# A new order of blocks and a sum that stays out of TensorE in layer 0 of a four-layer sparse graph network

## The chip, the cores and the metric

The kernel runs on one core of one Trainium2 chip. The metric is the device time of one execution in microseconds, from the first to the last instruction and what lies around them; lower is better. Engines are called PE (TensorE), DVE (VectorE), ACT (ScalarE), POOL (GpSimd) and SP (SyncE) in the profile.

## The reference

Four layers of graph attention run over 4096 nodes with 256 features each. An adjacency matrix of 4096 by 4096 integers says who is whose neighbour; it is symmetric, has ones on its diagonal, and each row has only a handful of ones.

```python
h = relu(layernorm(x));  x = x + L0(h, adj)   # 4 heads of 64, then elu
h = relu(layernorm(x));  x = x + L1(h, adj)   # 1 head, h @ W + att @ h
h = relu(layernorm(x));  x = x + L2(h, adj)   # 4 heads
h = relu(layernorm(x));  x = x + L3(h, adj)   # 4 heads, q k v

def L0(h, adj):
    Wh = (h @ W).reshape(n, 4, 64)
    e = leaky_relu(s_i[:, None] + s_j[None, :], 0.2)   # s_i, s_j: Wh times two vectors
    alpha = softmax(where(adj == 0, -inf, e), axis=1)
    return elu(einsum('ijh,jhd->ihd', alpha, Wh).reshape(n, 256))
```

## The kernel before

The kernel works on lists of neighbours instead of the matrix. Its first part (`lists`) scans the matrix, makes a list of up to 24 neighbours for every node, and sorts the nodes by the length of their lists. The sorted nodes lie in 32 blocks of 128, one node to a partition. `CAPS` gives the most neighbours that a node of each block may have: 23 in block 0, 14 in block 1, down to 3 in block 31.

Layer 0 begins inside that first part: while the matrix is scanned, the first 6 neighbours (`EARLY`) of every node are fetched and summed (`early`). What is left of layer 0 is its late part, which `layer(0)` runs once all lists are there. `slots(0, b)` is `CAPS[b] - 6`, at least 0: 17, 8, 7, 6, 6, 5, 5 for blocks 0 to 6, 4 for 7 to 9, 3 for 10 to 14, 2 for 15 to 18, 1 for 19 to 22, and 0 for blocks 23 to 31. Those last nine have no late neighbours: their early sum only has to be divided by the sum of its weights.

`layers` calls `reload` and then `layer` for each of the four layers. `reload` has SyncE load, one after the other: the lists of blocks 0 and 1, the lists of blocks 30 and 31, the rows (`rx`: features, early sum, its greatest score, its source score and the sum of its weights, 262 KB a block) of the first four blocks in the order of work, the lists of blocks 2 to 29, and the rows of the other 28 blocks. VectorE then makes three small tables from the lists (L708, L715, L717).

The order of work is written out by hand: within these functions each engine runs its instructions in the order of the program, and only semaphores make one engine wait for another. `layer` goes through the blocks in `ORDER`: 0, 31, 1, 30, 2, 29 and so on, a long list and a short one in turn. In each of its 32 steps:

- `fill` issues on GpSimd the gathers (L755) of the blocks up to four steps ahead (`AHEAD`), one gather of 128 rows for each slot, into a ring buffer. A gather of layer 0 reads the table of layer 0.
- `scores` (L913 to L952) makes the weights of the block's neighbours on VectorE, with the exponential on ScalarE. It does nothing for a block without slots.
- `weigh` (L974 to L1042) takes the sum. For a block with slots VectorE multiplies its own early sum (L1014) and the gathered rows (L1028) by their weights, and TensorE adds them up in PSUM by matmuls with the identity (L1019, L1038). A float32 matmul stands in the profile as two instructions. For a block without slots only L977 (reciprocal), L1014 and L1019 are left.
- `settle` of the block two steps back: ScalarE takes the exponential of the sum (L1052, L1053), VectorE makes elu of it and adds x (L1063, L1064), then the statistics of the next layer norm (L569, L570, L576).
- the norm of the block three steps back: four small VectorE instructions (L579 to L585), relu on ScalarE (L732), transposes on TensorE (L740), a copy on ScalarE (L742) and the product with layer 1's weights on TensorE (L748).
- `third` of the block four steps back: VectorE adds the product to x (L1080), ScalarE copies two small pieces (L1081, L1082), and GpSimd sends the rows to the table of layer 1 (L765).

In a step the program order is: gathers, exponential of the block two back, norm of the one three back, scores of this one, third of the one four back, rest of the settlement, product, weigh. GpSimd's queue holds gathers and sends in that order. Layer 1 gathers from the whole table of layer 1, so its first gather follows layer 0's last send.

Of the kernel before, what the change touches and what calls it, by code (L numbers as in the profile page):

```python
# [9 lines left out]
F32 = mybir.dt.float32  # L10
# [4 lines left out]
ALU = mybir.AluOpType  # L15
# [4 lines left out]
P = 128  # L20
D = 256
# [27 lines left out]
WL = W + TOPK  # L49

ORDER = [b for k in range(16) for b in (k, 31 - k)]

RING = 36 * 512
AT_ONCE = 8
# [15 lines left out]
class Sparse:  # L70
# [614 lines left out]
    def reload(self):  # L685

        nc, tc, nt, n = self.nc, self.tc, self.nt, self.n
        by_place = self.placed.rearrange("(b p) k -> p b k", p=P)
        near = self.near = self.big.tile([P, nt, 32], U32, name="s_near")
        for a, b in ((0, 2), (nt - 2, nt), (2, nt - 2)):  # L690
            back = nc.sync.dma_start(
                out=near[:, a:b, 0 : TOPK + 1],
                in_=by_place[:, a:b, OWN : OWN + TOPK + 1].bitcast(U32),
            )
            if a == 0:
                for i in self.sent:
                    tc.add_manual_dep(
                        back.ins, i.name,
                        mybir.DependencyInfo(
                            mybir.DependencyClass.Sync, mybir.DependencyReason.DATA  # L700
                        ),
                        reason="every row",
                    )
            for k in {0: [], nt - 2: ORDER[:4], 2: ORDER[4:]}[a]:
                nc.sync.dma_start(out=self.rx[k], in_=self.placed[ts(k, P), 0:OWN])

        self.own_f = self.big.tile([P, nt], F32, name="s_own_f")
        nc.vector.tensor_copy(self.own_f, near[:, :, TOPK])  # L708

        where = self.big.tile([P, nt], F32, name="s_place_of")  # L710
        nc.gpsimd.iota(
            where, pattern=[[P, nt]], base=0, channel_multiplier=1,
            allow_small_or_imprecise_dtypes=True,
        )
        nc.vector.tensor_copy(near[:, :, TOPK - 1], where)  # L715
        self.away = self.big.tile([P, nt, TOPK], F32, name="s_away")
        nc.vector.tensor_scalar(  # L717
            self.away, near[:, :, 0:TOPK], float(n), FAR, ALU.is_ge, ALU.mult
        )
# [86 lines left out]
    def layer(self, l):  # L806


        nc, nt, vs = self.nc, self.nt, {}
        wide = (W, WL, W, 2 * D)[l]  # L810
        slots = RING // wide
        ring = self.ring[:, : slots * wide].rearrange("p (k w) -> p k w", w=wide)
        todo, held, at = list(ORDER), {}, 0
        made = []

        def fill(i):
            nonlocal at
            while todo and nt - len(todo) <= i + AHEAD:
                j = todo[0]
                K = self.slots(l, j)  # L820

                room = K + (K % 2 if l > 1 else 0)
                s = (at if at + room <= slots else 0) if K else 0
                if any(s < e and b < s + room for b, e in held.values()) or (
                    l == 3 and len(held) > 3
                ):
                    return
                todo.pop(0)
                if l == 3:
                    vs[j] = self.pool.tile([P, D], F32, name=f"s_vself_{j}", tag="vself", bufs=5)  # L830
                    nc.sync.dma_start(out=vs[j], in_=self.tab[3][ts(j, P), D:])
                k0 = EARLY if l == 0 else 0
                for k in range(K):
                    at_k = self.near[:, j, k0 + k : k0 + k + 1]
                    self.fetch(ring[:, s + k, :], self.tab[l], at_k)
                held[j] = (s, s + room)
                at = s + room if K else at

        sums, behind, turning, rows = {}, {}, {}, {}

        def settle(c, parts=(0, 1)):

            if 0 in parts and c in sums:
                behind[c] = self.settle(l, c, sums.pop(c), made)
                next(behind[c])
            if 1 in parts and c in behind:
                next(behind[c])

        def norm(d):

            if l < 3 and d in behind:
                turning[d] = self.turned(self.pool, next(behind.pop(d)), f"{l + 1}_{d}")
                next(turning[d])

        def product(d):
            if d in turning:
                rows[d] = self.advance(l + 1, d, next(turning.pop(d)), made)
                next(rows[d])

        def third(d):  # L860
            if d in rows:
                next(rows.pop(d), None)
            for send in made:
                self.send(*send)
            made.clear()

        S, N = (0, 1) if l == 1 else (2, 3)
        for i in range(nt):
            fill(i)
            b, c, d, e = (ORDER[k] if k >= 0 else None for k in (i, i - S, i - N, i - N - 1))  # L870
            if S:
                settle(c, (0,))
            norm(d)
            g = ring[:, held[b][0] : held[b][1], :]
            p = self.scores(l, b, self.rows[b], g[:, : self.slots(l, b), :])
            third(e)
            if S:
                settle(c, (1,))
            product(d)
            sums[b] = self.weigh(l, b, vs.pop(b) if l == 3 else self.rows[b][:, 0:D], g, p)  # L880
            del held[b]
            if not S:
                settle(b)
        z, y, x, w = ORDER[-1:-5:-1]
        if S:
            settle(y)
            norm(x)
            third(w)
            product(x)
            settle(z)  # L890
            norm(y)
            third(x)
            product(y)
        norm(z)
        third(y)
        product(z)
        third(z)
# [72 lines left out]
    def weigh(self, l, b, me, g, p):  # L970

        nc, pool = self.nc, self.pool
        H = 1 if l == 1 else 4
        K = self.slots(l, b)  # L974
        tot = pool.tile([P, H], F32, name=f"s_t_{l}_{b}", tag="t", bufs=3)
        if K == 0:
            nc.vector.reciprocal(tot, self.before[b])  # L977
            mine = tot
        else:
            by_head = p[:, : K + 1, :].rearrange("p k h -> p h k")  # L980
            if l == 0:
                was = pool.tile([P, H], F32, name=f"s_was_{b}", tag="was", bufs=2)
                nc.vector.tensor_tensor(was, p[:, K, :], self.before[b], ALU.mult)
                nc.vector.tensor_reduce(tot, by_head[:, :, :K], AX.X, ALU.add)
                nc.vector.tensor_tensor(tot, tot, was, ALU.add)
            else:
                nc.vector.tensor_reduce(tot, by_head, AX.X, ALU.add)  # L987
            nc.vector.reciprocal(tot, tot)  # L988
            nc.vector.tensor_tensor(  # L989
                by_head, by_head, tot.unsqueeze(2).to_broadcast([P, H, K + 1]), ALU.mult  # L990
            )
            mine = p[:, K, :]
# [15 lines left out]
        if pairs and not full:  # L1008
            mev = g[:, K, v0 : v0 + D]
        else:  # L1010
            mev = pool.tile([P, D], F32, name=f"s_me_{l}_{b}", tag="me", bufs=3)
        if full:
            nc.vector.tensor_scalar(mine, mine, 0.5, None, ALU.mult)  # L1013
        nc.vector.tensor_tensor(  # L1014
# [121 lines left out]
class Net:  # L1136
# [341 lines left out]
    def dot_attention(self, wq, bq, wk, bk, wv, bv):  # L1478
        nc, tc, nt, n, nb = self.nc, self.tc, self.nt, self.n, self.nb
        scale = 1.0 / 8.0  # L1480
        with ExitStack() as ctx:
# [88 lines left out]
            for b in range(nb):  # L1570
# [45 lines left out]
                while waiting:  # L1616
                    weigh()
# [58 lines left out]
```

## Time and profile before

| | |
|---|---|
| three timed runs | 1837.8, 1838.98, 1839.6 us; median 1838.98 |
| the profiled execution | 1841.32 us, span 1839.6 us |
| busy: PE, DVE, ACT, POOL | 994.8, 1379.9, 423.7, 1184.8 us |
| late part of layer 0: first gather issued | 432.3 us |
| late part of layer 0: last send issued | 655.5 us |
| layer 1: first gather issued | 658.8 us |
| DVE, PE, ACT, POOL busy from 430 to 660 | 153, 129, 78, 123 us |

All times inside the execution are counted from the start of the span. Busy time is the sum over instructions, an average over stages that have different limits, so a stage has to be looked at by itself. In the lines of a timeline the first number is the start, the second the length in us; square brackets hold the idle time of the engine before it and what ended it. An instruction of a form such as `128x256 f32` works on 128 partitions with 256 float32 each.

### The profile page before, as it was taken

The numbers are of one execution on the slowest core, as the hardware profiler recorded it, in microseconds if no ns is written. First come the engines' busy times: TensorE is split into PE (matmuls) and PEld (weight loads), VectorE is DVE, ScalarE is ACT, GpSimd is POOL, SyncE is SP. The second block draws the span as 40 slices with busy tenths as digits, with TensorE's granted clock in tenths as the row PEclk, the third lists the DMA queues.
The fourth block names the chain that finished last, engine by engine and source line by source line (L and its number), as shares of the span: only waits on it lengthen the run. The fifth ranks groups of instructions, "written<-read, shape, count | busy, mean of one in ns | idle before, by whom it ended". The sixth has DMA issues, their size and how long they took to land. (4 is left out here: it accounts for less than half of the span.)

```text
span 1839.6 us, 14362 instructions
## 1 busy us (share of the span) xinstructions
PE 994.8 (54%) x2569; PEld 481.7 (26%) x2569; DVE 1379.9 (75%) x3900; ACT 423.7 (23%) x1240; POOL 1184.8 (64%) x1324
## 2 busy tenths in 40 slices
PE   4878787750666611222232167788785344565555
PEld 3523232220455400111111023343342111221122
DVE  6899989850688808888888257888885587887777
ACT  5864435000244401111111002222222000000000
POOL 1067756676566357777776477777772577776774
PEclk9988889875788855555555588889987676777777
DMA  9899877348533134444444344444443577666763
GB/s 319 281 394 363 287 259 254 97 148 242 168 87 88 51 84 128 131 132 130 132 132 121 69 111 133 134 135 131 136 131 97 156 215 210 208 208 181 209 205 108
DMA packets 123017, 312.89 MB, mean 170 GB/s; under 512 B 31236, under 2 KB 49671, under 8 KB 122920
## 3 DMA queue, kind: packets, MB, share of 16 engines
q0 software_dynamic: 68064, 207.46, 39.7%
q1 hardware_dynamic: 54856, 104.44, 16.2%
q14 instruction: 73, 0.60, 0.1%
q8 instruction: 24, 0.39, 0.1%
HBM read 276.80 MB, written 35.00 MB: 169 GB/s over the span
## 5 line engine op out<-in xcount | busy, mean ns | idle before, releaser
L755 POOL DMA_INDIRECT s_ring<-s_tab,s_near x924 | 883.8, 956 | 356.7 <-issue 190.4
L1033 PE MATMUL s_acc<-s_ring,s_ident 128*128 128x512 f32 x588 | 319.5, 697 | 183.3 <-issue 95.0
L1033 PEld LDWEIGHTS s_acc<-s_ring,s_ident 128*128 128x128 f32 x588 | 130.5, 228 | 368.2 <-issue 245.5
L755 POOL DMA_INDIRECT s_g<-s_tab,s_keep x192 | 183.2, 954 | 64.3 <-issue 57.0
L483 DVE MAX8 s_cand<-s_pt 128x8 f32<-128x256 f32 x512 | 181.6, 417 | 16.4 <-PE s_pt L481 15.9
L1028 DVE TENSOR_TENSOR s_ring<-s_ring,s_shares 128x2048 f32<-128x2048 f32 (+7 forms) x121 | 187.5, 1573 | 0.0
L740 PE MATMUL s_pht<-s_ident,s_h 128*128 128x128 f32 x128 | 34.3, 361 | 248.0 <-ACT s_h L732 248.0
L748 PE MATMUL s_ps<-s_we_l,s_ht 128*128 128x264 f32 x256 | 113.4, 586 | 79.2 <-ACT s_ht L742 79.2
L999 DVE SCALAR_TENSOR_TENSOR s_acc<-s_ring,s_p,s_acc 128x256 f32<-128x256 f32 x277 | 135.7, 490 | 9.7
L261 ACT ACTIVATE s_low<-s_raw 128x1024 fp8e4<-128x1024 int32 x128 | 134.2, 1050 | 21.3 <-DMA s_raw<-in_adj_dram 18.1
L556 PE MATMUL s_ae<-s_g,s_ident 128*128 128x512 f32 x192 | 113.7, 688 | 36.5 <-DVE s_g L547 36.5
L913 DVE TENSOR_TENSOR s_e<-s_ring,s_rx 128x8 f32<-128x8 f32 (+12 forms) x87 | 15.7, 181 | 148.0 <-DMA s_ring<-s_tab,s_near 143.0
L476 PE MATMUL s_pt<-s_low,s_mark 128*128 128x512 fp8e4 x256 | 107.7, 421 | 34.3 <-DVE s_cand L483 15.0
L748 PE MATMUL s_ps_kv<-s_wkv,s_ht 128*128 128x512 f32 x128 | 82.9, 782 | 73.6 <-ACT s_ht L742 73.6
L932 DVE TENSOR_TENSOR s_ring<-s_ring,s_shares 128x2048 f32<-128x2048 f32 (+7 forms) x48 | 81.1, 1690 | 47.8 <-DMA s_ring<-s_tab,s_near 31.5
L481 PE MATMUL s_pt<-s_places,s_stands 128*128 128x512 bf16 x256 | 106.5, 416 | 1.4 <-DVE s_stands L453 1.4
L952 ACT ACTIVATE s_shares<-s_e 128x32 f32<-128x32 f32 (+8 forms) x87 | 17.4, 200 | 387.8 <-DVE s_e L945 340.2
L575 ACT ACTIVATE s_y<-s_mv,s_eps 128x1 f32<-128x1 f32 x96 | 28.3, 294 | 294.0 <-DVE s_mv L570 294.0
L740 PEld LDWEIGHTS s_pht<-s_ident,s_h 128*128 128x128 f32 x128 | 18.3, 172 | 287.9 <-ACT s_h L732 271.9
L748 PEld LDWEIGHTS s_ps<-s_we_l,s_ht 128*128 128x128 f32 x256 | 63.0, 272 | 110.0 <-ACT s_ht L742 100.1
L935 DVE TENSOR_REDUCE s_e<-s_ring 128x32 f32<-128x2048 f32 (+7 forms) x48 | 81.2, 1692 | 1.7
L1021 PE MATMUL s_acc<-s_me,s_ident 128*128 128x512 f32 x60 | 42.8, 803 | 70.8 <-DVE s_me L1014 67.2
(193 smaller groups left out, 1673.4 us busy)
## 6 DMA issues: line engine op xcount, KB each, us to landing
s_raw<-in_adj_dram SPq DMA_DIRECT2D x128, 512.0 KB, 7.8
s_ring<-s_tab,s_near POOLq DMA_INDIRECT x924, 3.0
s_rx<-s_placed SPq DMA_DIRECT2D x32, 262.0 KB, 8.0
s_tab<-s_kv SPq DMA_DIRECT2D x32, 256.0 KB, 2.8
s_tab<-s_keep SPq DMA_DIRECT2D x8, 528.0 KB, 6.8
s_tab<-s_rx SPq DMA_DIRECT2D x32, 132.0 KB, 2.3
s_keep<-in_x_dram SPq DMA_DIRECT2D x8, 512.0 KB, 4.1
s_vself<-s_tab SPq DMA_DIRECT2D x32, 128.0 KB, 2.9
```

The costliest lines, as they stand in the source:

```text
L261: nc.scalar.activation(low[r][:, ts(h, n // 4)], raw.pop(q), AF.Copy, saturate=False, accum_out=self.sums[:, r, h : h + 1],)
L476: nc.tensor.matmul(pt, lhsT=self.mark, rhs=lo[:, ts(g, IB)], start=True, stop=False)
L481: nc.tensor.matmul(pt, lhsT=self.stands[:, g, :], rhs=self.places, start=False, stop=True)
L483: nc.vector.max(out=cand[:, g * (IB // CH) + k, :], in_=pt[:, ts(k, CH)])
L556: nc.tensor.matmul(acc, lhsT=self.ident, rhs=g[:, :, k, 0:D], start=False, stop=(k == E - 1))
L748: self.nc.tensor.matmul(ps[:, :width], lhsT=ht[:, c, :], rhs=w[:, c, :], start=(c == 0), stop=(c == KC - 1),)
L755: return self.nc.gpsimd.indirect_dma_start(out=out, out_offset=None, in_=table[:, :], in_offset=bass.IndirectOffsetOnAxis(ap=idx, axis=0),)
L932: nc.vector.tensor_tensor(kq, kq, q.unsqueeze(1).to_broadcast([P, m, D]), ALU.mult)
L935: nc.vector.tensor_reduce(e[:, k0 : k0 + m, :], kq.rearrange("p k (h d) -> p k h d", h=4), AX.X, ALU.add)
L999: nc.vector.scalar_tensor_tensor(acc, g[:, k, 0:D], p[:, k, :], acc, ALU.mult, ALU.add)
L1028: nc.vector.tensor_tensor(v, v, p[:, k0 : k0 + m, :].unsqueeze(3).to_broadcast([P, m, H, D // H]), ALU.mult)
L1033: nc.tensor.matmul(both, lhsT=self.ident, rhs=g[:, k : k + 2, v0 : v0 + D], start=(k == 0 and not full), stop=(k + 2 >= K),)
```

## The change

Layer 0's late part gets an order of its own, `FIRST`: 31, 30, 29, 28, 0, then 27, 1, 26, 2, 25, 3 and so on to 15, 13, and 14 at the end. The other layers keep `ORDER`. The rows are loaded in the new order too, five of them instead of four ahead of the lists of blocks 2 to 29. A block without slots no longer goes through TensorE: `weigh` returns the product of L1014 in SBUF, and `settle` reads it there. The buffer of these products has four places instead of three, since such a block holds its place until `settle` is done. The early return also skips `self.turns += 1` (L995), so `turns`, which picks one of two halves of the PSUM tile for the weights (L951), counts only blocks with slots in layer 0.

```diff
 ORDER = [b for k in range(16) for b in (k, 31 - k)]
+
+FIRST = [31, 30, 29, 28, 0] + [b for k in range(1, 14) for b in (28 - k, k)] + [14]
...
-            for k in {0: [], nt - 2: ORDER[:4], 2: ORDER[4:]}[a]:
+            for k in {0: [], nt - 2: FIRST[:5], 2: FIRST[5:]}[a]:
                 nc.sync.dma_start(out=self.rx[k], in_=self.placed[ts(k, P), 0:OWN])
...
-        todo, held, at = list(ORDER), {}, 0
+        order = ORDER if l else FIRST
+        todo, held, at = list(order), {}, 0
...
-            b, c, d, e = (ORDER[k] if k >= 0 else None for k in (i, i - S, i - N, i - N - 1))
+            b, c, d, e = (order[k] if k >= 0 else None for k in (i, i - S, i - N, i - N - 1))
...
-        z, y, x, w = ORDER[-1:-5:-1]
+        z, y, x, w = order[-1:-5:-1]
...
         if K == 0:
+
             nc.vector.reciprocal(tot, self.before[b])
-            mine = tot
+            mev = pool.tile([P, D], F32, name=f"s_me_{l}_{b}", tag="me", bufs=4)
+            nc.vector.tensor_tensor(
+                mev.rearrange("p (h d) -> p h d", h=H), me.rearrange("p (h d) -> p h d", h=H),
+                tot.unsqueeze(2).to_broadcast([P, H, D // H]), ALU.mult,
+            )
+            return mev
...
-            mev = pool.tile([P, D], F32, name=f"s_me_{l}_{b}", tag="me", bufs=3)
+            mev = pool.tile([P, D], F32, name=f"s_me_{l}_{b}", tag="me", bufs=4)
```

## The prediction

> **What bounds the kernel now.** I read the page first. VectorE is busy 75% of the span, more than any other engine, but that is an average over the list building and four layers, and the chain that ended last covers only the last 32 us (from 1807.6). So I cut the stage that the change touches, layer 0's late part, into windows.
>
> ```profile
> 443.00:464.00 21.00, 0.00 (x0) 0.00 (x0) 0.49 (x2) 0.00 (x0) 14.77 (x16) 0.50 0.99 271
> 464.00:480.00 16.00, 11.98 (x38) 9.24 (x38) 8.41 (x21) 0.57 (x2) 12.23 (x13) 0.66 0.91 325
> 520.00:540.00 20.00, 12.86 (x55) 9.72 (x56) 18.14 (x72) 10.06 (x38) 12.10 (x13) 0.99 0.31 88
> 620.00:640.00 20.00, 12.43 (x48) 9.13 (x47) 18.21 (x83) 9.74 (x36) 3.90 (x4) 0.88 0.09 31
> ```
>
> The columns are length, then busy us of PE, PE weight load, VectorE, ScalarE, GpSimd, the granted TensorE clock, the DMA share and GB/s. From 520 to 640 VectorE is busy 18 of each 20 us and the rest is gaps between instructions: it is the bound. From 443 to 464 it does nothing while GpSimd issues gathers and the DMA engines are full. The timeline of VectorE says what it waits for (start, length, then idle time before and releaser):
>
> ```profile
> 442.81 0.56 DVE L717 TENSOR_SCALAR s_away<-s_near 128x768 f32<-128x768 uint32 x1
> 463.88 0.23 DVE L913 TENSOR_TENSOR s_e<-s_ring,s_rx 128x68 f32<-128x68 f32 x1 [20.51 <-DMA s_ring<-s_tab,s_near]
> 480.53 0.43 DVE L1063 SCALAR_TENSOR_TENSOR s_ex<-s_ex,s_rx 128x256 f32<-128x256 f32 x1 [7.32 <-ACT s_ex L1053]
> 494.45 0.42 DVE L1080 TENSOR_TENSOR s_rx<-s_rx,s_ps 128x256 f32<-128x256 f32 x1 [3.92 <-PE s_ps L748]
> 517.57 0.42 DVE L1080 TENSOR_TENSOR s_rx<-s_rx,s_ps 128x256 f32<-128x256 f32 x1 [2.68 <-PE s_ps L748]
> ```
>
> 20.5 us go by until block 0's 17 gathers have landed, 7.3 us until ScalarE has block 0's sum, which waits for TensorE, and 3.9 and 2.7 us for TensorE's product. Later waits are small (0.55, 0.39, 0.39) until the tail. TensorE's own timeline explains three of them:
>
> ```profile
> 469.21 10.42 PE L1038 MATMUL s_acc<-s_ring,s_ident 128*128 128x256 f32 x34 [0.86 <-DVE s_ring L1028]
> 485.81 6.77 PE L1038 MATMUL s_acc<-s_ring,s_ident 128*128 128x256 f32 x16 [1.50 <-DVE s_ring L1028]
> 522.62 2.86 PE L1038 MATMUL s_acc<-s_ring,s_ident 128*128 128x256 f32 x12 [0.69 <-DVE s_ring L1028]
> ```
>
> Block 0's sum takes 10.4 us, and block 1's 16 instructions take 0.42 us each where a later block's 12 take 0.24: the granted clock is 0.50 until about 474, 1.00 from 476 to 483, and 0.50 again from 486 to 492. GpSimd's timeline gives the stage's two ends:
>
> ```profile
> 432.29 0.98 POOL L755 DMA_INDIRECT s_ring<-s_tab,s_near  x1 [1.77 <-DMA s_near<-s_placed]
> ...
> 655.55 0.97 POOL L765 DMA_INDIRECT s_tab<-s_rx,s_near  x1 [2.33 <-ACT s_rx L1082]
> 658.77 0.99 POOL L755 DMA_INDIRECT s_ring<-s_tab,s_near  x1 [2.25 <-DMA s_tab<-s_rx,s_near]
> ```
>
> Layer 1's first gather waits for layer 0's last row. So whatever moves that row moves everything after it, one for one.
>
> [...] the DMA share is 0.99 while SyncE's loads and GpSimd's gathers overlap, so the order of the loads can't make the gathers land much sooner. [...] L1064 with a PSUM operand takes 424 ns, L1063 with SBUF alone 418. So I count nothing for where VectorE reads the sum.
>
> **The change part by part.** CAPS minus 6 gives the gathers left in layer 0: 17, 8, 7, 6, 6, 5, 5 for blocks 0 to 6, then 4 to 1, and none for 23 to 31, 93 in all, as before.
>
> *TensorE bypass.* Nine blocks lose two matmul instructions each (379 to 590 ns the pair in TensorE's timeline), off VectorE's path: 0. ScalarE's exponential of an SBUF tile costs at most what L1053 shows over L1052 (417 against 388 ns), and ScalarE is half idle: 0. The fourth "me" buffer removes no wait that I find, and that `turns` now skips these blocks only changes which half of the share buffer a block uses: 0.
>
> *Loads.* Five row loads instead of four stand before the long list load on SyncE. At 0.47 us per issue and 262 KB against some 370 GB/s (0.7 us), L708 starts about 1 us later, near 443.5. That has cover: the moved work needs 8 us and is done by about 452, 12 us before block 0's gathers land. GpSimd's queue begins with the same 25 gathers for blocks 0 and 1, so I keep 463.9 for block 0, with ±1.5 us for the shared DMA engines. That rows load one by one is seen: L913 at 463.88 reads block 0's row while SyncE issues loads until 471.9.
>
> *Work moved ahead of 463.9.* For a block without gathers VectorE needs, from start to start: 0.55 us for L977 and L1014 (502.29 to 502.83), 1.67 for L1063 to L576 (510.85 to 512.51), 0.75 for L579 to L585, 0.33 for L1080. Before block 0's scores the new program order has four weighings (2.2), two settlements (3.3) and two norms (1.5): **7.0 us** leave the busy stretch.
>
> *From 463.9 on.* In program order: scores of 0 (1.2), row of 31 (0.33), settle 29 (1.67), weigh 0 (6.08 as at 465.52 to 471.60), norm 29 (0.75), row of 30 (0.33), settle 28 (1.67), weigh 27 (0.55), norm 28 (0.75), scores of 1 (1.0). That is 14.3 us, to 478.2. The 0.43 us wait for block 0's shares now lies under the row of 31 and settle 29, and the 7.3 us wait before L1063 is filled. What is late next is the row of 29 (L1080): its transposes stand behind block 0's matmuls in TensorE's queue. These begin 2.1 us later (row of 31 and settle 29 come first), so they end between 480.4[...] and 481.7. Transposes, ScalarE's copy and the product take 2.2 us more, as at 492.41 to 494.42. The new wait is 4.4 to 5.7 us; I take 5.0. Behind it on VectorE stands block 0's settlement, behind ScalarE's copy stand the exponentials of block 0, and on GpSimd the send of 29 and then block 4's six gathers. These leave GpSimd by about 499 and are needed near 515, so they have cover.
>
> *Rest of the layer.* Both orders then take blocks 2, 3, 4 with an empty one between. From block 5 on the partner has a gather (22, 21, 20...), which puts about 2 us more VectorE work between a product's start and its use, so the waits of 0.55, 0.39 and 0.39 go: 1.3. The waits of 3.92 and 2.68 belong to cold bursts. Warm, they would be about 0.9 and 0.3, 5.4 less. In the new order TensorE has the products of 29 and 28 between block 0 and block 1, where it idled 3.5 us, so a warm burst is likelier than before, not sure. I count half, 2.7.
>
> *Tail.* The last block has 3 gathers instead of 2: 0.27 us of VectorE and two more matmul instructions, -0.7.
>
> Sum: 7.0 + 0.4 + 7.3 + 1.3 - 5.0 + 2.7 - 0.7 = **13.0 us** saved. The profiled execution took 1841.3 (span 1839.6), so 1828.3; the three timed runs have a median 2.3 lower, so **1826.0**.
>
> **The rivals.**
> 1. *TensorE takes the gain back.* Block 0's burst stays at 0.42 us for all 34 instructions (14.3 us) and blocks 1 and 3 stay cold. The row of 29 then waits about 4.5 us longer and the 2.7 is lost: a gain near 6, 1833. For it: the cold stretches seen before. [...]
> 2. *Nothing measurable*: the gathers of block 0 land up to 6 us later, because the loads before them changed and the DMA engines are full, on top of cold bursts: within 3 us of before, about 1838. Against: the same bytes are ahead of them but for one load.
> 3. *Slower.* TensorE stays cold through the layer, because its work is spread thinner from the start. Layer 0 has about 232 sums at 0.42, 128 products at 0.53 and 64 transposes at 0.3 us: 184 us, more than VectorE's 160. It would end near 665 instead of 655.5, so about 1848. [...]
> 4. *It doesn't do what it says*: the first weighing waits until all rows have landed (about 480), so nothing is moved early and the layer ends some 10 us later, 1849. The early start of L913 all but excludes it.
>
> **How the numbers follow.** Forecast 0.64; rival 1 0.20; rival 2 0.09; rival 3 0.05; rival 4 0.02. A 0.2% difference is 3.7 us, about what a measurement of this kernel can tell from no change. Faster gets the forecast and most of rival 1 with a little of rival 2's spread, 0.85; same 0.08; slower 0.07. Range: with both bursts warm, the short wait and gathers 1.5 us earlier the gain is 18 (1821); with both cold, the long wait, no gain from the partners and gathers 1.5 us late it is 6 to 7 (1832.5). With rival 1 and a spread of 1 us in the runs: 1820.5 to 1834.
>
> **What would show it.** Right: VectorE works on L1014, L1063 and L1080-type lines from about 444 to 452 and idles only some 12 us before block 0's L913, still near 464; the 7.3 us wait at L1063 is gone, and an L1080 wait of 4 to 6 us stands near 483; last send near 642 to 643; layers 1 to 3 keep their lengths. Wrong: block 0's L913 later than 466, L1080 waits after 484 longer than 6 us in sum, or a later layer that changes its length by more than 2 us.

## The result, and the profile after

The changed kernel took 1823.85 us (median of four runs, 1820.8 to 1824.1), the kernel before 1839.29: a ratio of 0.9914 (0.9900 to 0.9929), 15.4 us less. The profiled execution took 1824.07 us with a span of 1822.3.

Lines have moved in the changed kernel: L916 is the old L913 (scores), L981 and L983 the weighing of a block without slots (old L977, L1014), L1028 the old L1019, L1037 the old L1028, L1047 the old L1038, L1062 the old L1053 (the exponential), L1072 and L1073 the old L1063 and L1064, L1089 the old L1080 (the row), L744 the old L742 (the copy), L750 the old L748 (the product).

One group of four runs below was made on a chip on which the kernel before itself took 2176 us; those runs are not compared with any others.

The same windows of the changed kernel, but 600 to 620 as the last, since the layer now ends at 641 (length, then busy us of PE, PE weight load, VectorE, ScalarE, GpSimd, granted clock, DMA share, GB/s):

```profile
443.00:464.00 21.00, 3.21 (x8) 1.92 (x8) 7.61 (x32) 4.63 (x13) 14.58 (x16) 0.50 1.00 256
464.00:480.00 16.00, 12.13 (x44) 9.62 (x45) 12.80 (x40) 4.08 (x16) 8.62 (x9) 0.74 0.88 320
520.00:540.00 20.00, 14.78 (x51) 10.33 (x49) 17.26 (x70) 8.33 (x30) 14.18 (x15) 0.83 0.35 102
600.00:620.00 20.00, 11.99 (x43) 8.64 (x43) 18.24 (x79) 9.30 (x34) 3.90 (x4) 0.89 0.12 37
```

VectorE now does 7.6 us of work from 443 to 464, where it did 0.5, and 12.8 instead of 8.4 from 464 to 480. From 520 on it is busy for 17 to 18 us in 20, as before. Its timeline:

```profile
443.21 0.56 DVE L719 TENSOR_SCALAR s_away<-s_near 128x768 f32<-128x768 uint32 x1
443.68 0.17 DVE L981 RECIPROCAL s_t<-s_rx 128x4 f32<-128x4 f32 x1
...
451.11 0.16 DVE L587 SCALAR_TENSOR_TENSOR s_rn<-s_mv,s_rn 128x1 f32<-128x1 f32 x1
463.47 0.23 DVE L916 TENSOR_TENSOR s_e<-s_ring,s_rx 128x68 f32<-128x68 f32 x1 [12.20 <-DMA s_ring<-s_tab,s_near]
...
480.77 0.42 DVE L1089 TENSOR_TENSOR s_rx<-s_rx,s_ps 128x256 f32<-128x256 f32 x1 [2.90 <-PE s_ps L750]
...
493.44 0.42 DVE L1089 TENSOR_TENSOR s_rx<-s_rx,s_ps 128x256 f32<-128x256 f32 x1 [2.03 <-PE s_ps L750]
...
504.37 0.42 DVE L1089 TENSOR_TENSOR s_rx<-s_rx,s_ps 128x256 f32<-128x256 f32 x1 [0.71 <-PE s_ps L750]
516.22 0.42 DVE L1089 TENSOR_TENSOR s_rx<-s_rx,s_ps 128x256 f32<-128x256 f32 x1 [1.69 <-PE s_ps L750]
527.10 0.42 DVE L1089 TENSOR_TENSOR s_rx<-s_rx,s_ps 128x256 f32<-128x256 f32 x1 [0.99 <-PE s_ps L750]
```

The early work runs from 443.7 to 451.3. VectorE goes on with block 0's scores, once its gathers have landed, at 463.5 (463.9 before), and 12.2 us of idle time are left ahead of them. The wait of 7.3 us at the settlement of block 0 is gone; the row of 29 waits 2.9 us in its place. TensorE and GpSimd:

```profile
467.41 2.13 PE L750 MATMUL s_ps<-s_we_l,s_ht 128*128 128x264 f32 x4 [14.13 <-ACT s_ht L744]
469.33 1.06 PE L1028 MATMUL s_acc<-s_me,s_ident 128*128 128x256 f32 x2
470.31 8.58 PE L1047 MATMUL s_acc<-s_ring,s_ident 128*128 128x256 f32 x34
```

```profile
431.71 0.98 POOL L757 DMA_INDIRECT s_ring<-s_tab,s_near  x1 [1.71 <-DMA s_near<-s_placed]
...
641.09 0.97 POOL L767 DMA_INDIRECT s_tab<-s_rx,s_near  x1 [2.33 <-ACT s_rx L1091]
644.32 0.99 POOL L757 DMA_INDIRECT s_ring<-s_tab,s_near  x1 [2.26 <-DMA s_tab<-s_rx,s_near]
```

I call the time from layer 0's first gather to its last send the stage. It was 655.55 - 432.29 = 223.3 us and is 641.09 - 431.71 = 209.4: 13.9 us less. From block 0's scores on, VectorE's busy time fell from 152.5 to 146.7 us and its idle time from 39.1 to 31.0. What follows layer 0 (from layer 1's first gather to the end of the span) took 1180.8 us before and 1178.0 after. Over the ten profiled executions of the table below it lies between 1177.8 and 1182.5, with no order in it that follows the changes, so I take those 2.9 us for chance.

### The profile page after: what moved, and what is told of

Its sections match the earlier page's. It is cut to its first block, busy times and chain, and to the rows that moved or that the text cites. A ratio compares the mean times of both kernels' runs of the same rounds, so it can differ in the third digit from the quotient of the medians.

```text
span 1822.3 us, 14325 instructions
## 1 busy us (share of the span) xinstructions
PE 991.5 (54%) x2551; PEld 476.5 (26%) x2551; DVE 1379.5 (76%) x3900; ACT 424.5 (23%) x1240; POOL 1185.3 (65%) x1324
## 5 line engine op out<-in xcount | busy, mean ns | idle before, releaser
L1037 DVE TENSOR_TENSOR s_ring<-s_ring,s_shares 128x2048 f32<-128x2048 f32 (+7 forms) x121 | 187.4, 1572 | 0.0
L742 PE MATMUL s_pht<-s_ident,s_h 128*128 128x128 f32 x128 | 34.3, 361 | 247.9 <-ACT s_h L734 247.9
L750 PE MATMUL s_ps<-s_we_l,s_ht 128*128 128x264 f32 x256 | 115.6, 596 | 92.5 <-ACT s_ht L744 92.5
L916 DVE TENSOR_TENSOR s_e<-s_ring,s_rx 128x8 f32<-128x8 f32 (+12 forms) x87 | 15.7, 181 | 140.1 <-DMA s_ring<-s_tab,s_near 135.3
L750 PE MATMUL s_ps_kv<-s_wkv,s_ht 128*128 128x512 f32 x128 | 79.2, 750 | 69.9 <-ACT s_ht L744 69.9
L750 PEld LDWEIGHTS s_ps<-s_we_l,s_ht 128*128 128x128 f32 x256 | 64.3, 277 | 123.9 <-ACT s_ht L744 113.7
L742 PEld LDWEIGHTS s_pht<-s_ident,s_h 128*128 128x128 f32 x128 | 18.3, 172 | 287.8 <-ACT s_h L734 271.8
L502 POOL TENSOR_SCALAR s_ids<-s_top 128x23 f32<-128x23 f32 x32 | 10.1, 314 | 108.7 <-DVE s_top L493 108.4
```

What stands on the lines that cost most here:

```text
L750: self.nc.tensor.matmul(ps[:, :width], lhsT=ht[:, c, :], rhs=w[:, c, :], start=(c == 0), stop=(c == KC - 1),)
L1037: nc.vector.tensor_tensor(v, v, p[:, k0 : k0 + m, :].unsqueeze(3).to_broadcast([P, m, H, D // H]), ALU.mult)
```

## The experiments

The theory: VectorE bounds the stage, so the gain is the work that is moved into its wait for block 0's gathers, and the wait for block 0's sum that is now covered. The rivals: the bypass of TensorE carries the gain, or the order of the loads does. A second question was the clock: why the new wait was 2.9 us where 5.0 were expected. No run takes away the cover of block 0's sum alone; what it is worth is read from the timelines. Each ratio in the table is to the kernel before of the same series (medians 1837.5 to 1839.3 us), so medians of different series compare only roughly.

| kernel | stage, us | idle before block 0's scores | median, us | ratio to before |
|---|---|---|---|---|
| before | 223.3 | 20.5 | 1839.3 | |
| changed | 209.4 | 12.2 | 1823.85 | 0.9914 (0.9900 to 0.9929) |
| order alone | 207.5 | 11.4 | 1826.5 | 0.9931 (0.9915 to 0.9947) |
| bypass alone | 224.6 | 20.7 | 1841.6 | 1.0012 (1.0004 to 1.0020) |
| loads as before | 209.5 | 14.2 | 1825.9 | 0.9935 (0.9919 to 0.9951) |
| seven first | 199.5 | 0.2 | 1816.35 | 0.9882 (0.9863 to 0.9901) |
| spare sum | 206.5 | 13.6 | 1825.5 | 0.9933 (0.9919 to 0.9946) |
| seven first, order alone | 197.6 | 0.2 | 1814.9 | 0.9874 (0.9856 to 0.9892) |
| two first | 218.5 | 19.4 | 1835.05 | 0.9977 (0.9967 to 0.9987) |
| warm array | 207.6 | 11.6 | 1827.5 | 0.9936 (0.9916 to 0.9957) |

**Order alone.**

```diff
         if K == 0:
             nc.vector.reciprocal(tot, self.before[b])
-            mev = pool.tile([P, D], F32, name=f"s_me_{l}_{b}", tag="me", bufs=4)
...
-            return mev
+            mine = tot
```

> The new order without the bypass: blocks without slots go through TensorE again. Theory (the gain is VectorE work moved into the wait for block 0's gathers, and cover for block 0's sum): 14 to 15.5 us under the kernel before, within 1.5 us of the changed kernel; the layer's first gather to last send near 209 us. Rival (the bypass carries the gain, because it clears TensorE's queue): less than 8 us under the kernel before, and the wait for the row of 29 (2.9 us in the changed kernel) longer.

Measured: 12.6 us under the kernel before (1826.5 against 1839.15), and a stage of 207.5 us, shorter than the changed kernel's. The wait for the row of 29 is 2.87 us, as in the changed kernel. The gain is below the 14 to 15.5 us expected. The median is 2.7 us over the changed kernel's, outside the 1.5 us that I gave it and the other way round from the stage; the two intervals overlap. The rival, a gain under 8 us and a longer wait, is out.

**Bypass alone.**

```diff
-            for k in {0: [], nt - 2: FIRST[:5], 2: FIRST[5:]}[a]:
+            for k in {0: [], nt - 2: ORDER[:4], 2: ORDER[4:]}[a]:
...
-        order = ORDER if l else FIRST
+        order = ORDER
```

> The bypass in the old order, loads as before. Theory: within 2 us of the kernel before; VectorE still waits 20 us for block 0's gathers and 7 us for its sum. Rival (the bypass carries the gain): more than 8 us under the kernel before.

Measured: 2.4 us over the kernel before, by the interval 0.7 to 3.7 us. VectorE's timeline has both large waits of the kernel before:

```profile
463.42 0.23 DVE L916 TENSOR_TENSOR s_e<-s_ring,s_rx 128x68 f32<-128x68 f32 x1 [20.73 <-DMA s_ring<-s_tab,s_near]
...
479.25 0.42 DVE L1072 SCALAR_TENSOR_TENSOR s_ex<-s_ex,s_rx 128x256 f32<-128x256 f32 x1 [6.51 <-ACT s_ex L1062]
```

So the gain comes from the order. By itself the bypass saves nothing and may cost a little.

**Loads as before.** Only the first of the two edits above.

> The changed kernel with the rows loaded in the old order (0, 31, 1, 30 ahead of the long list load, 29 and 28 behind it). Theory: the early work has 12 us of cover, so rows of 29 and 28 that come some us later cost nothing: within 1 us of the changed kernel, only VectorE's idle time before block 0's scores shrinks. Rival (the order of loads carries part of the gain, through the time at which block 0's gathers land or the first blocks start): 3 us or more over the changed kernel.

Measured: a stage of 209.5 us against 209.4. The median is 2.0 us over the changed kernel's, more than the 1 us expected, but with overlapping intervals. The order of the loads is worth nothing in the stage. The expectation missed one point: the idle time before block 0's scores grew, to 14.2 us instead of shrinking. With four rows instead of five ahead of the list load, VectorE makes its tables 9.2 us after the first gather instead of 11.2, so the early work starts those 2.0 us sooner, and rows of 29 and 28 behind the list load held nothing up.

**Seven first.**

```diff
-FIRST = [31, 30, 29, 28, 0] + [b for k in range(1, 14) for b in (28 - k, k)] + [14]
+FIRST = [31, 30, 29, 28, 27, 26, 25, 0] + [b for k in range(1, 13) for b in (25 - k, k)]
```

> Seven blocks without slots ahead of block 0 instead of four. Theory: 12.2 us of idle time are left before block 0's scores; three more blocks of 3.3 us each fill 9.9 of it, so 8 to 10 us under the changed kernel, some 1815 us, with about 2 us of idle time left before block 0's scores. Rival (the stage is now held by TensorE's waits or by GpSimd's sends, which come ahead of block 1's gathers): under 3 us of gain over the changed kernel, with new waits of VectorE after block 0.

Measured: a stage of 199.5 us, 9.9 shorter than the changed kernel's. The median (1816.35) is 7.5 us below the changed kernel's, a little less than the 8 to 10 expected, and the two intervals only just meet (0.9901 and 0.9900). The rival, a gain under 3 us, is out. VectorE's timeline in the window:

```profile
450.35 0.42 DVE L1089 TENSOR_TENSOR s_rx<-s_rx,s_ps 128x256 f32<-128x256 f32 x1 [1.61 <-PE s_ps L750]
...
455.28 0.42 DVE L1089 TENSOR_TENSOR s_rx<-s_rx,s_ps 128x256 f32<-128x256 f32 x1 [1.66 <-PE s_ps L750]
...
460.22 0.42 DVE L1089 TENSOR_TENSOR s_rx<-s_rx,s_ps 128x256 f32<-128x256 f32 x1 [1.62 <-PE s_ps L750]
...
463.73 0.23 DVE L916 TENSOR_TENSOR s_e<-s_ring,s_rx 128x68 f32<-128x68 f32 x1 [0.24 <-DMA s_rx<-s_placed]
```

The window is more than full. Block 0's scores wait 0.24 us instead of the 2 us expected, and the profile puts that down to the load of a row, not to their gathers. The window holds three waits of 1.6 us for products that take TensorE 2.12 to 2.13 us each, as at a granted clock of 0.50 in the changed kernel (1.16 at 1.00), so a block takes 4.9 us there instead of 3.3. From the first gather to block 0's scores it is now 34.8 us against 31.8 in the changed kernel, 3.1 longer. From the scores to the last send it is 164.7 against 177.6, 12.9 shorter: 8.8 us of work and 4.1 of idle time. That the balance comes to 9.9, three times 3.3, is luck.

**Two first.** `FIRST` is 31, 30, 0, then 29, 1 and so on to 16, 14, and 15.

> Two blocks without slots ahead of block 0 instead of four. Theory (work moved ahead of block 0's scores counts one for one): only two weighings, 1.1 us, are left before block 0's scores instead of 7.0, and the wait for block 0's sum stays covered: 5 to 7 us over the changed kernel, a stage (first gather to last send of layer 0) of 214.5 to 216.5 us. Rival (only the cover between block 0 and block 1 counts, not what comes before block 0): within 2 us of the changed kernel's 209.4.

Measured: a stage of 218.5 us, 9.1 over the changed kernel's. The rival (within 2 us) is out, but the theory expected 5 to 7. VectorE, then TensorE:

```profile
464.51 0.23 DVE L916 TENSOR_TENSOR s_e<-s_ring,s_rx 128x68 f32<-128x68 f32 x1 [19.39 <-DMA s_ring<-s_tab,s_near]
...
483.07 0.42 DVE L1089 TENSOR_TENSOR s_rx<-s_rx,s_ps 128x256 f32<-128x256 f32 x1 [4.77 <-PE s_ps L750]
...
496.58 0.42 DVE L1089 TENSOR_TENSOR s_rx<-s_rx,s_ps 128x256 f32<-128x256 f32 x1 [2.90 <-PE s_ps L750]
```

```profile
470.96 10.23 PE L1047 MATMUL s_acc<-s_ring,s_ident 128*128 128x256 f32 x34 [0.86 <-DVE s_ring L1037]
```

From block 0's scores to the last send, VectorE is busy 151.8 us against the changed kernel's 146.7, which is 5.2 of the 9.1 (the work that is no longer moved), and idle 34.7 against 31.0, another 3.8. Part of that is seen: block 0's sum takes 10.2 us, much as before the change (10.4), and the row behind it waits 4.77 us instead of 2.90. As before the change, TensorE does no product just ahead of the sum.

**Warm array.** Ahead of block 0's scores:

```diff
             norm(d)
+            if l == 0 and i == 4:
+                junk = self.pacc.tile([P, IB], F32, tag="acc", name="s_junk")
+                for k in range(12):
+                    nc.tensor.matmul(
+                        junk, lhsT=self.ident, rhs=self.wkv[:, 0, :],
+                        start=(k == 0), stop=(k == 11),
+                    )
```

> The changed kernel with 12 more matmuls of 512 columns on TensorE ahead of block 0's sum, whose result nobody reads. Theory (the wait for the row of 29, 2.9 us, comes from the half clock in which block 0's sum begins): the granted clock is 1.00 throughout the sum, which ends 3 us or more earlier against the start of block 0's weighing, and the wait falls below 0.5 us; the stage is 2 to 3 us shorter than 209.4. Rival (the wait is ScalarE's copy and the product's own length): it stays over 2 us.

TensorE's timeline, the window of 464 to 470 (columns as above, clock third from the end) and VectorE's row of 29 (L1054 is the sum here, L1096 the row):

```profile
454.22 11.53 PE L880 MATMUL s_junk<-s_wkv,s_ident 128*128 128x512 f32 x24
467.97 1.16 PE L750 MATMUL s_ps<-s_we_l,s_ht 128*128 128x264 f32 x4 [2.22 <-ACT s_ht L744]
...
470.88 7.61 PE L1054 MATMUL s_acc<-s_ring,s_ident 128*128 128x256 f32 x34 [1.32 <-DVE s_ring L1044]
```

```profile
464.00:470.00 6.00, 3.34 (x11) 1.50 (x9) 5.60 (x18) 2.00 (x8) 4.47 (x6) 1.00 1.04 386
```

```profile
480.36 0.42 DVE L1096 TENSOR_TENSOR s_rx<-s_rx,s_ps 128x256 f32<-128x256 f32 x1 [1.92 <-PE s_ps L750]
```

At full clock from its first instruction to its last (1.00 also from 464 to 480) the sum takes 7.6 us instead of 8.6, and the wait falls by the same 1.0 us, to 1.9. That is neither the theory's wait below 0.5 us nor the rival's over 2, but much nearer the rival. The clock accounts for 1.0 of the 2.9 us; the rest is the sum's own length at full clock (34 instructions at 0.22 us) with the copy and the product behind it. The stage is 1.8 us shorter than the changed kernel's, 1.1 of it behind block 0's scores; the median, 1827.5, does not show it.

**Spare sum.** In the changed kernel, TensorE also does the matmul that each of the nine blocks no longer needs, into a tile that nobody reads:

```diff
+            spare = self.pacc.tile([P, 2, D], F32, tag="acc", name=f"s_spare_{l}_{b}")
+            nc.tensor.matmul(spare[:, 0, :], lhsT=self.ident, rhs=mev, start=True, stop=True)
             return mev
```

> The changed kernel, where TensorE also does the nine matmuls that the bypass removed, into a PSUM tile that nobody reads; the sums still bypass it. Theory (the bypass made the stage from first gather to last send about 2 us longer, 209.4 against 207.5 us with the order alone, because TensorE idles more and falls to half clock more often): the waits for rows at steps 8 to 14 (2.0, 0.7, 1.7, 1.0 us in the changed kernel) fall to about those of the order alone (0.5, 0, 0.8, 0.5), and the stage is 207 to 208 us. Rival (the sum is read more slowly from SBUF, or it is chance): the stage stays at 209 to 210 us with the same waits.

VectorE's rows (L1091 here), and then the second product behind block 0's sum on TensorE, first in the changed kernel, then here:

```profile
492.42 0.42 DVE L1091 TENSOR_TENSOR s_rx<-s_rx,s_ps 128x256 f32<-128x256 f32 x1 [0.62 <-PE s_ps L750]
505.66 0.42 DVE L1091 TENSOR_TENSOR s_rx<-s_rx,s_ps 128x256 f32<-128x256 f32 x1 [2.98 <-PE s_ps L750]
```

```profile
483.54 2.13 PE L750 MATMUL s_ps<-s_we_l,s_ht 128*128 128x264 f32 x4 [2.30 <-ACT s_ht L744]
...
483.99 1.16 PE L750 MATMUL s_ps<-s_we_l,s_ht 128*128 128x264 f32 x4 [2.15 <-ACT s_ht L744]
```

Measured: a stage of 206.5 us, 2.9 shorter with more work on TensorE, and a granted clock of 0.91, 0.92 and 1.00 in the 20 us stretches from 480 to 540, where the changed kernel has 0.74, 0.83 and 0.83. But the waits did not fall as expected: 2.03 fell to 0.62, and those of 0.71, 1.69 and 0.99 became one of 2.98. And the median is 1825.5, not below the changed kernel's.

Is the clock chance? The traces of the new order speak against it for the stretch just behind block 0's sum. The second product there takes 2.13 us in the changed kernel, loads as before and seven first, 1.64 in warm array and 1.47 in two first. It takes 1.16 in the three kernels in which TensorE does a matmul for a block without slots between the first product and the second: order alone, spare sum, and seven first with the order alone. The clock from 480 to 500 is 0.74 in the changed kernel, 0.76 in warm array and 0.83 in two first, and 0.91 to 1.00 in these three. As nobody reads the spare sum, it is the work on TensorE that matters, not where the sum is read. The timed runs have the same sign: their mean clock over the whole execution is 0.746 in the changed kernel and 0.745 with loads as before, 0.750 with the order alone and 0.752 with the spare sum. What it is worth in time is less sure. From block 0's scores to the last send the profiles have 177.6 us in the changed kernel and with loads as before, 175.8 with the order alone and 174.4 here; the medians do not show it.

**Seven first, order alone.** Both edits together.

> Seven blocks without slots ahead of block 0, and their sums through TensorE as before. Theory: the early work still fits into the window before block 0's scores, so the stage is that of seven first (199.5 us) or 1 to 2 us shorter, some 22 to 26 us under the kernel before. Rival (each early sum now waits for a cold TensorE inside the window, about 1 us each, and block 0's scores begin later): the stage is 2 us or more longer than 199.5.

Measured: a stage of 197.6 us, the shortest, and 1814.9 us, 22.6 under the kernel before, as the theory had it; the rival is out. Of the 1.9 us that the stage is shorter than with the bypass, 1.3 lie ahead of block 0's scores: two of the three waits for rows there are 0.7 us instead of 1.6. Against seven first with the bypass (1816.35) the intervals overlap. Its interval, 0.9856 to 0.9892, lies below the changed kernel's.

**Four runs on a slower chip.** Two first, warm array and spare sum were first run with the same edits, and expectations in nearly the same words, on the chip on which the kernel before took 2176 us, together with all nine blocks first:

> All nine blocks without slots ahead of block 0. Theory: the window before block 0's scores is full with seven, so two more only move block 0's scores later by about what they take off the end: a stage within 1.5 us of the 199.5 of seven first. Rival (more early blocks always help): 5 us or more below seven first, a stage of 194 or less. Second rival (block 0's sum, begun later and with fewer empty blocks after it, costs its cover): 3 us or more above seven first.

Nine first took 2180.1 us there (ratio 1.0015, 0.9998 to 1.0031). Two first took 2154.5, warm array 2155.8, spare sum 2161.8, all about 0.99 of the kernel before. A part of nine first's timeline on VectorE shows how that chip differs:

```profile
529.05 0.16 DVE L582 TENSOR_TENSOR s_y<-s_y 128x1 f32<-128x1 f32 x1 [0.91 <-DVE s_y L581]
530.45 0.16 DVE L584 SCALAR_TENSOR_TENSOR s_rn<-s_y 128x1 f32<-128x1 f32 x1 [1.24 <-issue]
531.84 0.16 DVE L587 SCALAR_TENSOR_TENSOR s_rn<-s_mv,s_rn 128x1 f32<-128x1 f32 x1 [1.24 <-DVE s_rn L584]
```

Three small instructions that follow each other on one engine start 1.4 us apart, where they start 0.2 us apart elsewhere. Whether nine first is better than seven on the other chips stays open.

## Why the prediction was right, point by point

- **The bound.** VectorE, as read. The stage became shorter by what VectorE no longer does or waits for after block 0's scores (5.9 us of work and 8.2 of idle time), and seven first took another 8.8 us of work off that stretch.
- **Work moved ahead, 7.0 us.** It took 451.27 - 443.68, less one wait of 0.51 for ScalarE's exponential: 7.1, of which VectorE is busy 6.5. The cover of 12 us was 12.2. Block 0's scores began at 463.5 (463.9 before).
- **The loads at no cost.** The list load is used 0.4 us later than before (442.9), 1.0 later counted from the first gather, as forecast, and loads as before changed the stage by 0.1 us.
- **The waits that go.** Those of 7.3 and 0.4 us are gone. From the partners that have a gather I expected 1.3; after the wait at 527 there is none until the tail.
- **The new wait, 4.4 to 5.7 us, taken as 5.0.** This term was mis-sized: 2.9, at 480.8, and the wait of 4 to 6 us near 483 that I named as a sign did not come. VectorE came to it at 477.9, as worked out (478.2). What ended early was TensorE's sum, at 478.9 instead of 480.4 to 481.7. First, it began at 470.3, where the forecast's 2.1 us later gives 471.3. Block 0's scores were 0.4 us early. And the 2.1 us left out that the wait of 0.43 us for block 0's shares is now covered: from scores to sum it was 5.3 us and is 6.8, so 1.5 later. Second, the sum took 8.6 us, where I had it end 9.1 to 10.4 us after its start. The granted clock reached 1.00 at about 472.3, 2.0 us into the sum; before, at about 474.9, 5.7 us into it. A product just ahead goes with a shorter sum in every trace: 8.4 to 9.2 us in six, against 9.6 (bypass alone), 10.2 (two first) and 10.4 (before) without one, and 7.6 at full clock (warm array). Third, transposes, copy and product took 1.9 us more instead of 2.2; the stretch that 2.2 was read from, 492.41 to 494.42, is 2.0.
- **The cold bursts, 2.7 us.** Mis-sized the other way: the waits of 3.9, 0.3 and 2.7 us became 2.0, 0.7, 1.7 and 1.0, so 1.5 us. The four add up to 5.4, not far under the 6 us that I named as a sign of being wrong. Counting half of what full clock would save was my estimate; the profile before did not show which bursts would come at 0.50. The error in the new wait is in part, and this one in the whole, about TensorE's clock, and they nearly cancel, 2.1 more and 1.2 less: that the sum came out so near is partly luck.
- **The bypass at 0.** Right within what the runs can tell, with a sign that I hadn't looked for: bypass alone is 0.7 to 3.7 us slower than the kernel before. I looked only at the 379 to 590 ns of TensorE's time that it saves and not at what they do for the clock.
- **The tail, 0.7 us.** From the end of the last weighing's products to the last send it took 15.2 us before and 15.5 after, and the weighing itself is 0.26 longer.
- **Layers 1 to 3 unchanged.** Taken together as expected, within the spread of 4.7 us that all these profiles have there; I did not time the layers one by one.

The forecast was 13.0 us; the stage gave 13.9 and the medians 15.4. The rivals fell: TensorE did not take the gain back, block 0's gathers were not later, and the clock did not stay at half (0.84 from 500 to 640, 0.86 before).

## What to carry to other kernels

When the bounding engine waits at the head of a stage for its first gathers, put the items that need none in front, and count how many fit: the window divided by the time for one item there, its own waits included. Here the window was 20 us. An item took 3.3 us of VectorE, but 4.9 where it waited for a product of 2.13 us at half clock, and seven put block 0's scores off by 3.1 us. Seven still did better than four; five and six were not run. Look also at what stands in the first long sum's queue behind it, since the wait there moved to the next product and didn't vanish (7.3 us at block 0's settlement, then 2.9 at the row of 29).

## What I had not expected

TensorE's instruction of 256 columns took 0.22 us in a burst at full clock (7.61 us for 34), so block 0's sum is bound by TensorE, not by VectorE's products of the gathered rows (4.8 us), even at full clock. And taking work off TensorE went with a lower granted clock (mean of the three 20 us stretches from 480 to 540: 0.80 in the changed kernel, 0.89 with the order alone, 0.94 with the spare sum), and with a longer stage in every such pair of profiles: 209.4 against 207.5 and 206.5, 224.6 against 223.3, 199.5 against 197.6. The timed runs show a longer time only for the bypass alone.
